# A row of edge scores made by VectorE transposes and broadcast transfers, and a first pair of plain products, in a two-layer graph attention kernel on Trainium2

## Chip, cores and metric

One core of one Trainium2 chip runs the whole kernel. Its engines work side by side, each through its own instructions in order: TensorE (PE, with its weight loads PEld), VectorE (DVE), ScalarE (ACT), GpSimd (POOL) and SyncE (SP), which issues nearly all transfers. The metric is the device time of one launch in microseconds (us); less is better.

## What is computed

x has 128 graphs of 128 nodes with 512 features; adj holds, for each graph, a 128x128 matrix of zeros and ones. Layer 0 is masked attention with eight heads of 64, layer 1 a graph attention with one head. Each layer adds its input and normalizes each node's features.

```python
# layer 0
q, k, v = x @ Wq + bq, x @ Wk + bk, x @ Wv + bv            # 8 heads of 64
attn = softmax(where(adj > 0, q @ k.T / 8, -1e9))          # per graph and head
x = layernorm(x + relu((attn @ v) @ Wo + bo))
# layer 1
Wh = x @ W
e = leaky_relu((Wh @ a1)[:, :, None] + (Wh @ a2)[:, None, :], 0.2)   # e_i + e_j
attention = softmax(where(adj == 0, -1e9, e))              # per graph
x = layernorm(x + elu(attention @ Wh))
```

All of it is float32.

## The kernel before

**Pairs.** Two graphs make a pair; there are 64 pairs, numbered p. The two graphs of a pair are the two row halves of one 256x512 matrix, and each of the products by Wq and Wk (`qk0` to `qk6`), Wv (`v0` to `v6`), Wo (`o0` to `o6`) and W (`w0` to `w6`) is a 2x2 block product with seven block products instead of eight. For that the blocks of the left side are added up by GpSimd (`x_sums`, `o_sums`, `z_sums`: four additions each, in `left_sums`), and the blocks of the weights once at the start (`sums_qk`, `sums_v`, `sums_o`, `sums_w`). The seven products share three PSUM banks, A, B and C: `PRODUCTS` lists for each the bank, the left block and the weight block. A product that adds to a bank has to wait until the partial sum in it has been read. The reads are called by the tag and the part: `qk_p1` and `qk_p1q` (ScalarE) read bank A after product 0, `qk_p6` and `qk_p7` (VectorE) read B after products 1 and 3, and `c11`, `c22`, `c21`, `c12` write the four blocks of the result. The same names with `v_`, `o_` and `w_` stand for the other three weights. For qk the 128x512 output takes eight 128x128 matmuls a product (each shows as two records); for v, o and w a product is two 128x256 matmuls.

**Steps of a pair.** `load_blocks` loads x in blocks (`xb`) and `x_transpose0/1` transposes it on VectorE into `xT`. After `qk` and `v` come `logits` (TensorE), `mask_logits0/1` and `max_logits0/1` (VectorE), `exp_logits`, `norm_logits` (ScalarE), and the transpose of the attention weights: `weights_t` (VectorE, 32x32 blocks, tile `prb`), `weights_out` (to HBM, `prd`) and `weights_in` (back as `prT`). `mix_values` (TensorE, tile `po`) and `mix_values_out` (ScalarE) lead to `o`, then `residual0`, `stats0`, `mean0`, `rstd0`, `shift0`, `norm0`. Layer 1 uses (attention @ x) @ W. W @ a1 and W @ a2 are folded at the start: `fold_a` (keys `sums_fold0/1`, 8 products on VectorE after a load of one half of `a` issued by GpSimd), `fold_t` (TensorE, `pwa`), `fold_out` (ScalarE, `wa_bc`). `edge_term0i` and `edge_term1i` (VectorE, L506) give the node columns e_i and e_j, `edge_row` makes a row of the column e_j, and then come `edge_sums` (ScalarE, L525), `edge_leaky`, `edge_mask`, `edge_max` (VectorE), `edge_exp`, the transpose `edges_t`, `edges_t_out`, `edges_t_in` (tiles `atb`, `atd`, `attT`), `mix_nodes` (TensorE, `pz`), `mix_nodes_out`, the products of `w`, the elu (`elu_exp`, `elu_low` on GpSimd, `elu_max`), `residual1`, the second normalization and `store`. The last pair transposes with TensorE instead of through HBM (`ppT`, `pat`).

**The row before.** The column is broadcast to 128 columns and transposed by TensorE into PSUM:

```python
for i in range(2):
    nc.tensor.transpose(ST["j", p][:, i, :], ej[:, i:i + 1].to_broadcast([P, P]), ident)
```

**The order.** It is written out by hand. `PLAN` gives each step a time, `PERIOD` the distance of two pairs, and all steps of all pairs are sorted by p * PERIOD + PLAN[key]; the numbers set only the order, in which every engine then gets its own instructions. In the steady state TensorE works on the products of several pairs in turn: `qk` and `v` of pair p+1 stand near `o` of pair p-1 and `w` of pair p-3. `BUFS` gives the number of buffers of each tile. One PSUM bank (tag `ps`, one buffer) is shared by `po`, `pj`, `pz` and `pwa`. The steps `sums_...` run once.

Of the kernel before, what the change touches and what calls it, by code (L numbers as in the profile page):

```python
# [14 lines left out]
N_BATCH = 128  # L15


PERIOD = 75.72
PLAN = dict(
    load_blocks=-145.14, x_transpose1=-53.4, x_transpose0=-35.51, sums_qk=-33.34, sums_fold1=-29.39, qk0=-27.1,  # L20
    x_sums=-23.88, qk_p1=-23.14, qk1=-22.39, fill_logits0=-21.87, qk_p1q=-21.45, qk2=-21.2, qk_c11=-20.29,
    qk_p6=-19.48, sums_v=-18.68, qk3=-17.99, load_adj=-17.97, mask=-17.48, qk_p7=-16.28, qk4=-15.67, qk5=-15.2,
    qk_c22=-12.6, qk6=-10.28, v0=-9.3, qk_c21=-4.36, qk_c12=-1.71, v_p1=-1.71, logits=0.0, fill_logits1=0.47,
    mask_logits0=2.51, max_logits0=3.23, v1=3.74, v2=5.42, v_p6=9.86, v3=10.28, mask_logits1=11.03, v_c11=11.14,
    v4=11.19, v_p7=11.39, v5=11.72, max_logits1=11.91, v_c22=12.76, exp_logits0=13.09, v6=13.11, v_c21=17.62,
    v_c12=24.79, sum_logits0=38.24, exp_logits1=39.15, sums_fold0=44.28, sum_logits1=44.73, norm_logits0=46.84,
    sums_fold_t1=51.88, sums_fold_out1=51.93, weights_t0=52.11, sums_fold_t0=54.57, norm_logits1=54.59,
    weights_t1=56.92, weights_out0=69.01, sums_fold_out0=71.24, weights_out1=72.35, weights_in0=73.55,
    mix_values0=75.07, mix_values_out0=75.62, weights_in1=76.59, mix_values1=77.67, sums_w=80.78,
    mix_values_out1=82.2, sums_o=82.43, o_sums=83.08, load_x1=83.6, fill_edges=94.56, o0=106.33, o_p1=107.8,  # L30
    o1=110.7, o_p6=113.29, o4=114.99, o3=115.54, o_p1l=115.68, o_p7=116.85, o2=117.07, o5=117.95, load_x0=119.48,
    o_c11=123.99, o_c22=124.53, o6=125.56, o_c21=125.62, residual01=129.31, o_c12=132.6, stats01=134.5,
    mean01=136.37, rstd01=136.65, shift01=136.91, residual00=138.02, stats00=142.08, mean00=142.88, norm01=143.34,
    rstd00=143.95, shift00=146.71, edge_term01=147.04, edge_term11=147.54, norm00=147.98, edge_term10=152.41,
    edge_term00=152.98, edge_row=160.06, edge_sums=163.14, edge_leaky=163.47, edge_mask=167.08, edge_max=171.62,
    edge_exp=173.19, edges_t=179.68, edges_t_out=188.05, edges_t_in=199.52, mix_nodes1=209.13,
    mix_nodes_out1=213.74, mix_nodes0=214.15, mix_nodes_out0=221.07, z_sums=225.48, w0=238.82, w_p1=240.45,
    w1=248.86, w2=249.67, w_p6=251.97, w3=255.0, w_c11=255.99, w_p7=256.03, w4=256.11, w_c22=259.18, w5=259.7,
    w6=259.92, edge_norm=261.55, w_c21=261.61, w_c12=264.14, elu_exp1=276.85, elu_low1=281.16, elu_exp0=304.17,
    elu_low0=304.34, elu_max0=329.44, elu_max1=330.72, residual10=333.57, stats10=338.98, mean10=339.98,  # L40
    residual11=340.94, rstd10=361.09, shift10=363.8, stats11=376.92, mean11=380.35, rstd11=388.98, shift11=391.45,
    finish0=399.29, store0=407.37, finish1=407.57, store1=460.65)

ENDS = {}

BUFS = dict(
    xb=2, adj=4, xT=2, sx=1, e1a512=1, e1b512=1, u2512=1, pr=2, mask=1, u3512=1, qT=2, kT=2, e1a256=2, t=2, scr=1,
    cw=6, u2256=1, u3256=2, cv=2, prb=2, x=2, prT=2, oT=2, so=1, e1b256=1, co=6, at=2, e=1, atb=1, attT=1, zT=2,
    sz=1)


@with_exitstack
def tile_two_graph_layers(ctx: ExitStack, tc: tile.TileContext, x, adj, wq, bq, wk, bk, wv, bv, wo, bo, w, a, out,
# [8 lines left out]
    nc = tc.nc  # L62
    P = 128
# [43 lines left out]
    make_identity(nc, ident)  # L107
    half = const.tile([P, 1], F32, tag="half", name="half")
    nc.gpsimd.memset(half, -0.5)

# [179 lines left out]
        left_sums("x", p, XT)  # L290

    def qk_product(p, j):
        if j == 0:
            BL["qk", p] = Blocks("qk", p, D)
        columns_product(BL["qk", p], wqk, "x", j)

    def with_bias(dst, src, bias):
        for f in range(NC):
            nc.scalar.activation(dst[:, f * P:(f + 1) * P], src[:, f * P:(f + 1) * P], AF.Identity,
                                 bias=bias[:, f:f + 1], scale=1.0)  # L300

    def qk_p1(p):
        b = BL["qk", p]
        b.e1k, b.e1q = b.tile("e1a"), b.tile("e1b")
        with_bias(b.e1k, b.bank["A"], bk_sb)

    def qk_p1q(p):
        b = BL["qk", p]
        with_bias(b.e1q, b.bank["A"], bqs)

    def qk_p6(p):
        b = BL["qk", p]
        b.u2 = b.tile("u2")
        nc.vector.tensor_add(b.u2, b.bank["B"], b.e1k)  # L314

# [183 lines left out]
    def edge_term(b, s):  # L499

        p, i = b // 2, b % 2
        store = (EI, EJ)[s]
        if p not in store:
            store[p] = small.tile([P, 2], F32, tag=f"e{s}", name=f"e{s}_{p}")
        scr = buf([P, D], F32, "scr", f"scr{s}_{b}")
        nc.vector.scalar_tensor_tensor(scr, X1[b], 1.0, wa_bc[s], op0=ALU.mult, op1=ALU.mult,  # L506
                                       accum_out=store[p][:, i:i + 1])


    def edge_row(p):  # L510

        ej = EJ.pop(p)
        ST["j", p] = ps.tile([P, 2, P], F32, tag="ps", name=f"pj_{p}")
        for i in range(2):
            nc.tensor.transpose(ST["j", p][:, i, :], ej[:, i:i + 1].to_broadcast([P, P]), ident)
# [5 lines left out]
    def edge_sums(p):  # L521
        e = ST["e", p] = buf([P, 2, P], F32, "e", f"e_{p}")
        j, ei = ST.pop(("j", p)), EI.pop(p)
        for i in range(2):
            nc.scalar.activation(e[:, i, :], j[:, i, :], AF.Identity, bias=ei[:, i:i + 1], scale=1.0)  # L525
# [168 lines left out]
```

## Time and profile before

| what | value |
|---|---|
| median of 3 runs | 2439.42 us (2438.52 to 2440.8) |
| the profiled execution | 2441.85 us, span 2440.1 us |
| mean granted TensorE clock | 0.990 |
| VectorE busy | 1881.5 us (77%) |
| ScalarE busy | 1570.9 us (64%) |
| GpSimd busy | 1497.0 us (61%) |
| TensorE busy in the first 40 us | 10.95 us |
| TensorE busy from 200 to 600 us | 400.00 us |
| TensorE busy in the last 60 us | 37.63 us |
| `pj` (L515) | 128 matmuls, 25.1 us busy, mean 278 ns |
| L506 (`edge_term`) | 128x512, 256 times, median 692 ns, at most 1253 ns |

A line of a timeline reads: start, us from first start to last end, engine, line of the kernel, operation, output <- inputs, shapes, count, and in brackets the idle time before it with what ended it. TensorE's instructions overlap: the time that one takes from the next is the distance of two starts. A line of waits reads: engine, tile and line that waited, what it waited for, total, times, longest. A line of transfer issues ends with the size of one and the median time from issue to landing.

### The profile page before, as it was taken

How to read it: one execution, taken by the hardware profiler on the slowest of the kernel's cores; microseconds unless marked ns; L12 is line 12 of the kernel's file. 1: busy time of each engine (PE TensorE's matmuls, PEld its weight loads, DVE VectorE, ACT ScalarE, POOL GpSimd, SP SyncE). 2: the span in 40 equal slices, each digit the busy share in tenths (PEclk: the TensorE clock that was granted, in tenths of full speed). 3: DMA queues.
4: the chain of work that ended last, by engine and by line, in shares of the span. 5: the costliest groups of instructions: out<-in, count | busy, mean ns of one | idle time of the engine just before them, and what ended most of it. 6: DMA issues, size and time to landing. Idle time of an engine off the chain costs nothing. (4 is left out here: it accounts for less than half of the span.)

```text
span 2440.1 us, 51873 instructions
## 1 busy us (share of the span) xinstructions
PE 2383.7 (98%) x17818; PEld 2156.8 (88%) x17818; DVE 1881.5 (77%) x3838; ACT 1570.9 (64%) x5510; POOL 1497.0 (61%) x1989
## 2 busy tenths in 40 slices
PE   4999999999999999999999999999999999999996
PEld 4899899899899998998998998998998989989985
DVE  4777877877877877877778778778778778778786
ACT  2666666667667666666666666666666676676674
POOL 1445665666666666666666656656656666666657
PEclk8999999999999999999999999999999999999998
DMA  5443443443443443443443444434434434434421
GB/s 130 113 107 101 108 120 104 114 120 97 118 123 92 118 126 93 115 121 101 112 118 99 120 113 104 120 108 110 120 100 115 122 92 119 127 92 116 121 82 53
DMA packets 305766, 267.14 MB, mean 109 GB/s; under 512 B 89760, under 2 KB 255392, under 8 KB 305504
## 3 DMA queue, kind: packets, MB, share of 16 engines
q1 hardware_dynamic: 304528, 261.98, 40.4%
q8 instruction: 143, 2.34, 0.4%
q10 hardware_dynamic: 640, 1.05, 0.2%
q14 instruction: 119, 0.97, 0.1%
q0 software_dynamic: 336, 0.79, 0.1%
HBM read 155.85 MB, written 107.87 MB: 108 GB/s over the span
## 5 line engine op out<-in xcount | busy, mean ns | idle before, releaser
L425 ACT ACTIVATE pr<-pr,nmax 128x128 f32<-128x128 f32 x1024 | 394.9, 393 | 0.0
L434 ACT ACTIVATE pr<-pr,tot 128x128 f32<-128x128 f32 x1024 | 314.6, 412 | 106.6 <-DVE tot L429 106.6
L271 POOL TENSOR_SCALAR rstd<-mv 128x1 f32<-128x1 f32 x256 | 112.0, 437 | 319.7 <-DVE mv L268 310.2
L604 POOL TENSOR_TENSOR cw<-cw,co 128x512 f32<-128x512 f32 x126 | 184.3, 1482 | 163.2 <-DVE cw L601 163.2
L255 PE MATMUL pBqk<-sx,wqk 128*128 128x128 f32 x2048 | 253.1, 277 | 18.6 <-issue 13.7
L255 PEld LDWEIGHTS pBqk<-sx,wqk 128*128 128x128 f32 x2048 | 247.0, 194 | 22.1 <-issue 18.9
L255 PE MATMUL pAqk<-xT,wqk 128*128 128x128 f32 x2048 | 251.9, 277 | 13.2 <-DVE xT L286 10.5
L598 POOL TENSOR_SCALAR t<-t 128x512 f32<-128x512 f32 x126 | 245.4, 1948 | 31.5 <-ACT t L594 31.5
L279 ACT ACTIVATE co<-co,nmean,rstd 128x512 f32<-128x512 f32 x128 | 104.2, 814 | 246.8 <-DVE kT L330 216.8
L255 PEld LDWEIGHTS pAqk<-xT,wqk 128*128 128x128 f32 x2048 | 245.8, 193 | 17.2 <-DVE xT L286 10.5
L255 PE MATMUL pCqk<-sx,wqk 128*128 128x128 f32 x2048 | 250.6, 276 | 0.0
L255 PEld LDWEIGHTS pCqk<-sx,wqk 128*128 128x128 f32 x2048 | 240.0, 193 | 0.0
L484 ACT ACTIVATE oT<-po,bv 128x128 f32<-128x128 f32 x512 | 146.3, 368 | 123.2 <-PE po L475 123.2
L506 DVE SCALAR_TENSOR_TENSOR scr<-co,wa_bc 128x512 f32<-128x512 f32 x256 | 201.8, 788 | 8.4 <-ACT co L279 3.2
L425 ACT ACTIVATION_READ_ACCUMULATOR pr<-pr,nmax 128x1 f32 x1024 | 198.1, 193 | 0.0
L444 DVE STREAM_TRANSPOSE prb<-pr 128x1024 f32<-128x1024 f32 x126 | 156.2, 1239 | 49.4 <-ACT pr L434 49.4
L410 POOL MEMSET pr<- 128x1024 f32 x128 | 121.6, 951 | 99.8 <-DVE prb L444 99.8
L414 DVE COPY_PREDICATED pr<-mask,s 128x1024 f32<-128x1024 int32 x128 | 173.1, 1352 | 4.3 <-PE s L402 4.2
L272 POOL TENSOR_TENSOR rstd<-rstd,half 128x1 f32<-128x1 f32 x256 | 159.5, 623 | 21.3
L419 DVE TENSOR_REDUCE nmax<-pr 128x8 f32<-128x1024 f32 x128 | 155.4, 1214 | 2.2
L314 DVE TENSOR_TENSOR u2qk<-pBqk,e1aqk 128x512 f32<-128x512 f32 x64 | 44.2, 690 | 144.3 <-PE pBqk L255 141.6
L150 POOL TENSOR_TENSOR sx<-sx,xT 128x256 f32<-128x256 f32 x63 | 46.1, 732 | 175.6 <-DVE xT L286 175.5
(155 smaller groups left out, 6144.1 us busy)
## 6 DMA issues: line engine op xcount, KB each, us to landing
prd<-prb SPq DMA_DIRECT2D x126, 512.0 KB, 2.9
prT<-prd SPq DMA_DIRECT2D x504, 128.0 KB, 3.6
xb<-in_x_dram SPq DMA_DIRECT2D x256, 128.0 KB, 4.3
x<-in_x_dram SPq DMA_DIRECT2D x128, 256.0 KB, 3.7
out_dram<-cw SPq DMA_DIRECT2D x128, 256.0 KB, 2.0
adj<-in_adj_dram SPq DMA_DIRECT2D x64, 128.0 KB, 2.3
atd<-atb SPq DMA_DIRECT2D x63, 128.0 KB, 1.8
attT<-atd SPq DMA_DIRECT2D x252, 32.0 KB, 1.9
```

The lines of the kernel that those rows point to most:

```text
L255: nc.tensor.matmul(out[:, f * P:(f + 1) * P], weight[:, b_i, c, f * P:(f + 1) * P], left_block(left, blk.pair, a_i, c), start=first and f ...
L272: nc.gpsimd.tensor_tensor(RSTD[key], RSTD[key], half, op=ALU.pow)
L410: nc.gpsimd.memset(PR[b], NEG)
L414: nc.vector.copy_predicated(PR[b], MASK[p][:, i, :].unsqueeze(1).to_broadcast([P, H, P]), ST.pop(("s", b)).rearrange("p j h k -> p (j h) k"))
L419: nc.vector.tensor_reduce(NMAX[b], PR[b], AX.X, ALU.max, negate=True)
L425: nc.scalar.activation(PR[b][:, h, :], PR[b][:, h, :], AF.Exp, bias=nmax[:, h:h + 1], scale=1.0, accum_out=TOT[b][:, h:h + 1])
L434: nc.scalar.activation(PR[b][:, h, :], PR[b][:, h, :], AF.Copy, scale=tot[:, h:h + 1])
L444: nc.vector.transpose(PRB[b].rearrange("p k h s -> p h k s"), PR.pop(b).rearrange("p h (k r) -> p h k r", r=32))
L484: nc.scalar.activation(OT[b][:, f, :], po[:, f, :], AF.Identity, bias=bv_sb[:, f:f + 1], scale=1.0)
L506: nc.vector.scalar_tensor_tensor(scr, X1[b], 1.0, wa_bc[s], op0=ALU.mult, op1=ALU.mult, accum_out=store[p][:, i:i + 1])
L598: side_engine(b // 2).tensor_scalar(t, t, 1.0, -1.0, op0=ALU.min, op1=ALU.add)
L604: side_engine(b // 2).tensor_tensor(Y[b], Y[b], X1.pop(b), op=ALU.add)
```

## The change

The two transposes of `edge_row` on TensorE go. The columns e_j are now accumulated into columns 0 and 32 of one of three 128x64 tiles that were filled with zeros once (`ej_blocks`); `edge_blocks` transposes such a tile in 32x32 blocks on VectorE, so that four partitions (0, 32, 64, 96) hold the row in pieces of 32 for both graphs; `edge_row` then issues four transfers on SP, each of which copies 64 numbers of one partition to all 128 partitions, 256 bytes each. `edge_sums` reads the row from SBUF instead of PSUM. For pair 0, Q and K come from eight plain products in four steps (`qk0` to `qk3`) in banks A, B, C and a fourth bank D, with the bias added by ScalarE when a product is read; `sums_qk` and `x_sums` are not needed for them. `PLAN`, `PERIOD` and `BUFS` are new, and with them the order of all steps: among others `sums_qk` and `sums_fold0` come later, `qk4` before `qk2`, `v1` before `mix_values0`, `v3` before `v2`, `edge_term00` between `mask_logits0` and `max_logits0`, and `weights_t1` after `qk1`.

```diff
@@ -15,38 +15,38 @@
 N_BATCH = 128
 
 
-PERIOD = 75.72
+PERIOD = 78.77
 PLAN = dict(
...
-    finish0=399.29, store0=407.37, finish1=407.57, store1=460.65)
+    load_adj=-214.28, load_blocks=-156.46, x_transpose0=-118.96, x_transpose1=-64.06, qk0=-36.02, x_sums=-35.84,
+    qk1=-32.98, qk_p1=-31.71, fill_logits0=-31.52, sums_v=-30.63, qk4=-28.65, qk_p6=-28.53, qk_p1q=-27.7,
+    qk2=-26.32, qk_c11=-24.89, qk3=-22.63, v0=-21.4, qk_p7=-19.94, qk_c22=-19.93, qk5=-14.75, qk6=-13.44,
+    qk_c21=-7.89, qk_c12=-7.85, sums_fold1=-6.69, v_p1=-4.73, v1=-4.54, fill_logits1=-1.85, mask=-1.24, v_p6=-0.29,
+    logits=0.0, mask_logits0=2.0, max_logits0=3.74, sums_fold_t1=4.13, v3=4.41, v_p7=4.43, v2=7.45, v4=9.21,
+    v_c11=9.21, mask_logits1=10.04, load_x1=10.32, v5=13.29, v_c22=14.67, exp_logits0=14.75, v_c21=15.09, v6=17.23,
+    v_c12=17.58, max_logits1=22.12, sum_logits0=24.06, norm_logits0=27.41, exp_logits1=33.3, sums_qk=38.84,
+    weights_t0=43.7, sum_logits1=43.78, sums_fold_out1=45.25, sums_fold0=46.53, norm_logits1=52.01,
+    weights_out0=53.62, weights_t1=55.61, sums_fold_t0=63.24, weights_out1=68.01, weights_in0=70.44,
+    sums_fold_out0=71.92, weights_in1=74.3, mix_values0=75.85, sums_w=78.52, mix_values_out0=80.72,
+    mix_values1=81.43, mix_values_out1=85.44, load_x0=87.17, sums_o=94.72, o_sums=101.64, o0=106.22, o_p1=113.64,
+    o1=113.67, o4=115.87, o_p6=116.22, o_p1l=117.15, o3=117.16, o_p7=117.32, o2=117.77, o_c11=118.24, o_c22=118.29,
+    o5=120.85, o6=121.7, o_c21=121.88, o_c12=122.76, residual01=122.76, stats01=122.82, mean01=123.85,
+    residual00=127.73, rstd01=128.28, shift01=128.77, stats00=130.31, norm01=131.24, mean00=131.45, rstd00=133.98,
+    edge_term01=134.39, shift00=135.59, edge_term11=137.39, norm00=140.45, edge_term10=144.28, edge_blocks=146.15,
+    fill_edges=152.96, edge_row=155.48, edge_term00=159.96, edge_sums=163.39, edge_leaky=169.07, edge_mask=175.0,
+    edge_max=179.3, edge_exp=184.85, edges_t=185.93, edges_t_out=188.28, edges_t_in=189.77, mix_nodes1=211.95,
+    mix_nodes_out1=218.25, mix_nodes0=220.51, mix_nodes_out0=222.79, z_sums=231.06, w0=248.23, edge_norm=250.39,
+    w_p1=253.84, w1=254.02, w2=254.75, w_p6=256.75, w3=258.71, w_c11=259.13, w4=262.95, w_p7=264.55, w5=268.2,
+    w_c22=268.29, w6=268.5, w_c21=269.01, w_c12=270.9, elu_exp1=288.36, elu_exp0=298.97, elu_low1=307.12,
+    elu_max1=314.12, elu_low0=326.19, elu_max0=338.66, residual10=340.21, stats10=349.64, mean10=349.96,
+    residual11=350.83, rstd10=358.93, stats11=386.25, mean11=395.88, shift10=413.33, rstd11=414.6, shift11=416.7,
+    finish0=436.56, finish1=440.87, store0=451.59, store1=492.12)
 
 ENDS = {}
 
 BUFS = dict(
-    xb=2, adj=4, xT=2, sx=1, e1a512=1, e1b512=1, u2512=1, pr=2, mask=1, u3512=1, qT=2, kT=2, e1a256=2, t=2, scr=1,
...
-    sz=1)
+    xb=2, adj=5, xT=3, t=2, scr=1, cw=6, sx=1, pr=2, qT=2, kT=2, mask=2, e1a256=1, u2256=1, cv=2, u3256=1, prb=1,
+    e1a512=1, e1b512=1, u2512=1, u3512=1, prT=2, oT=2, so=1, x=3, at=1, e1b256=1, co=6, ejr=1, e=1, atb=1, attT=1,
+    zT=2, sz=1)
 
 
 @with_exitstack
@@ -107,6 +107,10 @@
     make_identity(nc, ident)
     half = const.tile([P, 1], F32, tag="half", name="half")
     nc.gpsimd.memset(half, -0.5)
+
+    ej_blocks = [const.tile([P, 64], F32, tag=f"ej{k}", name=f"ejb_{k}") for k in range(3)]
+    for t in ej_blocks:
+        nc.gpsimd.memset(t, 0.0)
 
 
 
@@ -290,9 +294,29 @@
         left_sums("x", p, XT)
 
     def qk_product(p, j):
-        if j == 0:
+        if p == 0:
+            if j < 4:
+                qk_plain(j)
+            return
+        if ("qk", p) not in BL:
             BL["qk", p] = Blocks("qk", p, D)
         columns_product(BL["qk", p], wqk, "x", j)
+
+    def qk_plain(j):
+
+        if j == 0:
+            b = BL["qk", 0] = Blocks("qk", 0, D)
+            for bank in "ABC":
+                b.psum(bank)
+            b.bank["D"] = ps.tile([P, D], F32, tag="ps", name="pDqk_0")
+        banks, half, b_i = (("AB", 0, 0), ("AB", 1, 1), ("CD", 0, 5), ("CD", 1, 2))[j]
+        for i, bank in enumerate(banks):
+            out = BL["qk", 0].bank[bank]
+            for f in range(NC):
+                for c in range(2):
+                    nc.tensor.matmul(out[:, f * P:(f + 1) * P], wqk[:, b_i, c, f * P:(f + 1) * P],
+                                     left_block("x", 0, 2 * i + half, c), start=half == 0 and f == 0 and c == 0,
+                                     stop=half == 1 and f == NC - 1 and c == 1, skip_group_check=True)
 
     def with_bias(dst, src, bias):
         for f in range(NC):
@@ -301,15 +325,20 @@
 
     def qk_p1(p):
         b = BL["qk", p]
+        if p == 0:
+            return
         b.e1k, b.e1q = b.tile("e1a"), b.tile("e1b")
         with_bias(b.e1k, b.bank["A"], bk_sb)
 
     def qk_p1q(p):
         b = BL["qk", p]
-        with_bias(b.e1q, b.bank["A"], bqs)
+        if p:
+            with_bias(b.e1q, b.bank["A"], bqs)
 
     def qk_p6(p):
         b = BL["qk", p]
+        if p == 0:
+            return
         b.u2 = b.tile("u2")
         nc.vector.tensor_add(b.u2, b.bank["B"], b.e1k)
 
@@ -322,24 +351,35 @@
 
     def qk_p7(p):
         b = BL["qk", p]
+        if p == 0:
+            return
         b.u3 = b.tile("u3")
         nc.vector.tensor_add(b.u3, b.bank["B"], b.e1k)
 
     def qk_c22(p):
         b = BL["qk", p]
-        nc.vector.tensor_add(QK["k", 2 * p + 1], b.bank["C"], b.u3)
+        if p == 0:
+            with_bias(QK["k", 1], b.bank["D"], bk_sb)
+        else:
+            nc.vector.tensor_add(QK["k", 2 * p + 1], b.bank["C"], b.u3)
 
     def qk_c21(p):
         b = BL["qk", p]
-        nc.vector.tensor_add(QK["q", 2 * p + 1], b.bank["B"], b.e1q)
+        if p == 0:
+            with_bias(QK["q", 1], b.bank["B"], bqs)
+        else:
+            nc.vector.tensor_add(QK["q", 2 * p + 1], b.bank["B"], b.e1q)
 
     def qk_c12(p):
         b = BL["qk", p]
-        nc.vector.tensor_add(QK["k", 2 * p], b.bank["C"], b.u2)
+        if p == 0:
+            with_bias(QK["k", 0], b.bank["C"], bk_sb)
+        else:
+            nc.vector.tensor_add(QK["k", 2 * p], b.bank["C"], b.u2)
 
     def half_product(tag, p, j):
 
-        if j == 0:
+        if (tag, p) not in BL:
             BL[tag, p] = Blocks(tag, p, HALF)
         weight, left = dict(v=(wv_b, "x"), o=(wo_b, "o"), w=(w_b, "z"))[tag]
         rows_product(BL[tag, p], weight, left, j)
@@ -499,20 +539,24 @@
     def edge_term(b, s):
 
         p, i = b // 2, b % 2
-        store = (EI, EJ)[s]
-        if p not in store:
-            store[p] = small.tile([P, 2], F32, tag=f"e{s}", name=f"e{s}_{p}")
+        if s == 0 and p not in EI:
+            EI[p] = small.tile([P, 2], F32, tag="ei", name=f"ei_{p}")
+        acc = ej_blocks[p % 3][:, 32 * i:32 * i + 1] if s else EI[p][:, i:i + 1]
         scr = buf([P, D], F32, "scr", f"scr{s}_{b}")
-        nc.vector.scalar_tensor_tensor(scr, X1[b], 1.0, wa_bc[s], op0=ALU.mult, op1=ALU.mult,
-                                       accum_out=store[p][:, i:i + 1])
-
+        nc.vector.scalar_tensor_tensor(scr, X1[b], 1.0, wa_bc[s], op0=ALU.mult, op1=ALU.mult, accum_out=acc)
+
+
+    def edge_blocks(p):
+
+        EJ[p] = small.tile([P, 64], F32, tag="ej", name=f"ej_{p}")
+        nc.vector.transpose(EJ[p], ej_blocks[p % 3])
 
     def edge_row(p):
 
+        ST["j", p] = buf([P, 4, 64], F32, "ejr", f"ejr_{p}")
         ej = EJ.pop(p)
-        ST["j", p] = ps.tile([P, 2, P], F32, tag="ps", name=f"pj_{p}")
-        for i in range(2):
-            nc.tensor.transpose(ST["j", p][:, i, :], ej[:, i:i + 1].to_broadcast([P, P]), ident)
+        for v in range(4):
+            nc.sync.dma_start(ST["j", p][:, v, :], ej[32 * v:32 * v + 1, :].unsqueeze(1).to_broadcast([1, P, 64]))
 
     def fill_edges(p):
         AT[p] = buf([P, 2, P], F32, "at", f"at_{p}")
@@ -522,7 +566,8 @@
         e = ST["e", p] = buf([P, 2, P], F32, "e", f"e_{p}")
         j, ei = ST.pop(("j", p)), EI.pop(p)
         for i in range(2):
-            nc.scalar.activation(e[:, i, :], j[:, i, :], AF.Identity, bias=ei[:, i:i + 1], scale=1.0)
+            nc.scalar.activation(e[:, i, :].rearrange("p (v s) -> p v s", s=32), j[:, :, 32 * i:32 * i + 32],
+                                 AF.Identity, bias=ei[:, i:i + 1], scale=1.0)
 
     def edge_leaky(p):
         e = ST["e", p]
@@ -624,7 +669,7 @@
         if p > 1:
             at("load_adj", p, load_adj, p)
             at("load_blocks", p, load_blocks, p)
-        for fn in (edge_row, fill_edges, edge_sums, edge_leaky, edge_mask, edge_max, edge_exp,
+        for fn in (edge_blocks, edge_row, fill_edges, edge_sums, edge_leaky, edge_mask, edge_max, edge_exp,
                    edge_norm, edges_t, edges_t_out, edges_t_in):
             at(fn.__name__, p, fn, p)
         at("x_sums", p, x_sums, p)
```

More of the change, by code (lines that the diff above doesn't have):

```diff
@@ L15 @@
 N_BATCH = 128
-PERIOD = 75.72
+PERIOD = 78.77
 PLAN = dict(
[L20 to L41, printed above, removed]
-    finish0=399.29, store0=407.37, finish1=407.57, store1=460.65)
@@ L44 @@
+    elu_max1=314.12, elu_low0=326.19, elu_max0=338.66, residual10=340.21, stats10=349.64, mean10=349.96,
+    residual11=350.83, rstd10=358.93, stats11=386.25, mean11=395.88, shift10=413.33, rstd11=414.6, shift11=416.7,
+    finish0=436.56, finish1=440.87, store0=451.59, store1=492.12)
 ENDS = {}
 BUFS = dict(
-    xb=2, adj=4, xT=2, sx=1, e1a512=1, e1b512=1, u2512=1, pr=2, mask=1, u3512=1, qT=2, kT=2, e1a256=2, t=2, scr=1,
-    cw=6, u2256=1, u3256=2, cv=2, prb=2, x=2, prT=2, oT=2, so=1, e1b256=1, co=6, at=2, e=1, atb=1, attT=1, zT=2,
```

## The prediction

> **What bounds the kernel now.** I read the page's busy shares first, then its slices, TensorE's waits, and timelines of the start, of one pair in the middle and of the end.
>
> ```profile
> PE 2383.7 (98%) x17818; PEld 2156.8 (88%) x17818; DVE 1881.5 (77%) x3838; ACT 1570.9 (64%) x5510; POOL 1497.0 (61%) x1989
> PE   4999999999999999999999999999999999999996
> ```
>
> TensorE is the bound: every slice but the first and the last is full. Three things can matter: fewer TensorE instructions in the middle, a shorter start or end, new holes in the middle. Its waits (engine, line, releaser: total, times, longest):
>
> ```profile
> PE pBqk L255 <- issue: 13.7, 1, 13.7
> PE pAqk L255 <- DVE xT L286: 10.5, 1, 10.5
> PE pBqk L255 <- DVE wqk L130: 4.8, 1, 4.8
> ```
>
> Three waits at the start hold 29.0 us. The rest of the list is some 15 us, nearly all in the first 115 us and the last 65. The middle, on TensorE's timeline:
>
> ```profile
> 1028.21 1.03 PE L244 MATMUL pAv<-wv,xT 128*128 128x256 f32 x4
> 1029.08 0.38 PE L515 MATMUL pj<-ident,e 128*128 128x128 f32 x2
> 1029.30 1.03 PE L244 MATMUL pBv<-wv,sx 128*128 128x256 f32 x4
> ```
>
> Starts count here, since ends overlap. The two transposes of `edge_row` take 1029.30 - 1029.08 = 0.22 us of a pair's 36.94 (`e1bo` of `o_p1` starts at 1001.26 and again at 1038.20).
>
> **Part 1: the row leaves TensorE.** 62 of the 64 `pj` lie in the full stretch: 62 x 0.22 = 13.6 us less; the other two belong to the tail (part 3). What replaces them:
> - VectorE: one 128x64 stream transpose. The nearest row is the 128x256 one, 0.44; by width 0.15. VectorE is 77% busy and waits for TensorE just behind it (`qk_c21`), so it costs nothing; uncovered, at most 62 x 0.44 = 27.
> - SP: four issues at 0.45 (`attT`'s four take 1.80) of 32 KB each. The nearest landing has the same size in pieces of 128 B (last number: us to landing):
>
> ```profile
> attT<-atd SPq DMA_DIRECT2D x252, 32.0 KB, 1.9
> ```
>
> The Trainium skill, "DMA: Bandwidth & Descriptors", Specifications, speaks against the transfers: pieces under 512 B are read, modified and written instead of moved at line rate, and these have 256 B. The `attT` row, with smaller pieces, shows no such delay; were each landing doubled by it, 3.8, the wait below would still be hidden.
>
> Is the row in time? I laid the changed order along TensorE's start-to-start times of this trace (0.86 a 128x256 product, 1.79 an eight-matmul 128x128 one, 0.89 `pz`, 1.03 `po`, 1.99 `logits`). From a pair's `logits` at 0: `po` 2.0, `v3` 3.0, `v2`, `v4`, `w0` 5.7, `v5` 6.6, `v6` 7.4, six of w and `o0`, `o1` 14.3, `o5` 17.8, `qk0` 18.6, `o6`, `qk1` 21.3, `qk4`, `qk2` 24.8, `pz`, `qk3`, `v0` 29.3, `pz`, `qk5`, `qk6`, `v1` 34.6, `po` 35.5, end 36.7. ScalarE: `qk_p1` and `qk_p1q` to 22.6, `norm_logits1` (2.4) to 25.0; `weights_t1` to 26.4; its write takes 2.9, so `weights_in1` is issued to 31.5. `edge_blocks` ends at 31.6. The broadcasts are issued 31.6 to 33.4 and land near 35. ScalarE's `edge_sums` stands at 1.2 of the next period (37.9), behind `mix_values_out0`. Behind it wait `mix_values_out1`, `v_c11`, and through that `w0` at 5.7: a broadcast may take 7 us to land before `w0` is late. The slowest `xb` load took 6.5. What SP issues behind it (`load_blocks`, two `load_x`) moves by 1.8 and is needed 15 later.
>
> **Part 2: the first pair.** Before, VectorE's queue decided: `sums_fold1` waited for W in front of `qk_p6`, so product 4 of 7 started at 38.82, at half pace.
>
> ```profile
> 22.41 2.66 PE L255 MATMUL pAqk<-xT,wqk 128*128 128x128 f32 x16
> 38.82 3.75 PE L255 MATMUL pBqk<-sx,wqk 128*128 128x128 f32 x16 [13.75 <-issue]
> 75.52 1.09 PE L475 MATMUL po<-prT,cv 128*64 128x128 f32 x16
> ```
>
> ```profile
> 36.09 0.43 DVE L207 SCALAR_TENSOR_TENSOR wa_scr<-w,a_bc 128x256 f32<-128x256 f32 x1 [1.36 <-DMA w<-in_L_gnn_W_dram]
> 38.03 0.68 DVE L314 TENSOR_TENSOR u2qk<-pBqk,e1aqk 128x512 f32<-128x512 f32 x1
> ```
>
> After, the plain products need only both `xT` and Wq, Wk (the last Wk was there at 17.49): start 9.9, about 23 records at 0.22 and 105 at 0.11, end 27. The extra product (1.79) falls into time that was idle. But `sums_fold1` still stands on VectorE ahead of `mask`, `v_p6` and `mask_logits0`, and W comes when it came: TensorE does `v0`, `v1`, `logits` to about 33, and the rest starts at 38.0. Each step by its row:
> - VectorE: mask 0.2, `v_p6` 0.4, `mask_logits0` 1.4, max 1.1, `v_p7` 0.3, `mask_logits1` 1.3, `v_c22` 0.4. TensorE, cold: `pwa`, `v3` to `v6`, end 45.2.
> - VectorE's max to 46.9; ScalarE normalizes (2.4) to 49.5, second exp (3.1) to 52.6. GpSimd: `x_sums` of pair 1 to 48.2, and only then the load of the second row of `a`, which took 5.8 to land: 54.0. `sums_fold0` 4.2, `qk_p6` 0.6: 58.8.
> - `qk3` of pair 1 at 58.9, `v0`, `pwa`, `qk5`, `qk6`, `v1` (1.79 + 0.86 + 0.44 + 1.79 + 1.79 + 0.86 = 7.5): `po` of pair 0 at 66.5.
>
> Before, `po` stood at 75.52 with `v1` still to come. Gain 75.52 + 0.86 - 66.5 = 9.9. If the row of `a` lands earlier, the exponentials (52.8) decide: +1.2; if half pace hits `qk1` to `qk3` and `prT` (3.6 to land) holds `po`: -3. So 7 to 11.
>
> **Part 3: the tail.** Before, TensorE stood for `po` (1.38), `po` (1.68), `pj` (1.24) and later 3.76 at the last `pj`, ahead of `w0`. After, the last `ppT` and `pz` alternate and nothing stands ahead of `w0`: pair 61's w may start up to 3.6 earlier. But the last pair's row needs four issues and a landing (3.7) where `pj` took 0.5; part of that is covered by w, so 0.8 to 2.5 later. Gain -2 to 3.5; taken 1.5.
>
> **Part 4: the new order in the middle.** Where VectorE gates TensorE, a margin of 0.17 between its end and the product's start was free (`v_c22` 1032.58, `v6` 1032.75), 0.16 cost 0.07 (`w_p6` 1035.18, `w3` 1035.34). After, by the same sums, most margins are 0.18 to 0.26 and `qk0`'s is 0.14: about as before. But one step meets GpSimd. VectorE from `mask_logits0` (1.27 after `logits`, as at 49.64 and 50.91): 1.33, 0.10, `edge_term00` 0.73, max 1.13, `v_p7` 0.34, `mask_logits1` 1.33, so `edge_leaky` at 6.24. GpSimd's four `o_sums` start 2.37 after the second `po` (1026.22, 1028.59), at 4.4, 5.2, 5.9 and 6.6. A two-input VectorE operation that meets such a sum is held until it ends; the normal `edge_leaky` took 0.42, the last one
>
> ```profile
> 2410.91 0.79 DVE L529 SCALAR_TENSOR_TENSOR e<-e 128x256 f32<-128x256 f32 x1 [0.66 <-ACT e L525]
> 2410.70 0.72 POOL L152 TENSOR_TENSOR sz<-zT,sz 128x256 f32<-128x256 f32 x1
> ```
>
> So `edge_leaky` is held by the third sum: worth 6.5; `edge_norm` and `v_c22` follow, to 7.38; `v6` at 7.42 needs 0.16: 0.12 lost a pair, x 62 = 7.4 us. Ends: 0 (it comes before 5.9) and the first rival.
> `edge_term01` and `11` meet `elu_low1`: the one like case (L491 beside L598) took 1.02 instead of 0.66. 0.7 for both, hidden by the wait for `qk3`. The Trainium skill, "SBUF — State Buffer", has the loser of the shared port wait for the whole other instruction, which would be 1.7 and almost all of that cover; the row did not.
>
> **Sum.** 13.6 + 9.9 + 1.5 - 7.4 = 17.6. The profiled execution was 2441.85 (span 2440.1), 2.4 above the median 2439.42: 2424.2 for it, 2421.8 for the median.
>
> **Rivals.**
> - Slower: `edge_leaky` comes after 6.6 and is held by the fourth sum to 7.2. Then `v_c22` ends at 8.07 and `v6` loses 0.81 a pair, x 62 = 50: 2439 - 25 + 50 = 2464. It decides from 0.36 us of lateness in VectorE. For: `edge_term00` took 1.09, not 0.69, beside GpSimd's sums before. Against: here only 128x1 operations run beside it. 0.15.
> - Only part 1 counts, since W and the row of `a` set the start: 13.6 + 1.5 - 7.4 = 7.7, 2432. For: 38.03 stays. Against: what follows it is shorter. 0.12.
> - The broadcast lands after 7 us: each us more costs 62; at 8 it is 2484. Against: 1.9. 0.03.
> - My forecast, own range 2409 to 2430: 0.70.
>
> **Numbers.** Median 2421.8. Low end: start 11, no held `edge_leaky`, tail 3.5: 2411, and 3 for what I overlooked: 2408. High end: past 2432, to 2440, until two in ten are out. The runs lie within 2.3 us, so 0.2% (4.9) can be told from no change. Faster, from the forecast and half of the second rival: 0.76; within 0.2%: 0.06; slower: 0.18.
>
> **What would show it.** No `pj`; 36.7 to 36.9 between two `logits`; `edge_sums` without a wait for a DMA; `po` of pair 0 near 66.5; `edge_leaky` longer than 0.42 in every pair. I am wrong if TensorE's waits list `w0`, `v6` or `qk0` some sixty times beyond 0.2, or if the second row of `a` does not gate `sums_fold0`.

## The result, and the profile after

The changed kernel takes 2425.58 us (median of 4 runs, 2423.96 to 2427.27), the kernel before on the same chip 2440.11 (4 runs): 0.9941 times as long, 95% interval 0.9924 to 0.9958, 14.5 us less. The forecast was 2421.8 in 2408 to 2440. The profiled execution took 2427.27 with a span of 2425.5; before, 2441.85 and 2440.1. Both profiles lie 1.7 us above their medians, so their difference, 14.6, is close to that of the medians.

The page's busy shares and TensorE's slices:

```profile
PE 2375.7 (98%) x17706; PEld 2149.5 (89%) x17706; DVE 1846.5 (76%) x3897; ACT 1558.2 (64%) x5514; POOL 1473.9 (61%) x1992
PE   6999999999999999999999999999999999999996
```

TensorE is still the bound, and only the two end slices are not full. So the span can be cut at the starts of `logits`, one per pair: the stretch to the fourth, the sixty periods from there to the last, and the end. The forecast's terms are put on the same cuts (`v1` of the next pair now stands ahead of `logits`, so its 0.86 us counts less for the start and more for the end; the two pairs outside the sixty make up the end's last 0.2).

| stretch | before | after | change | forecast |
|---|---|---|---|---|
| start to the fourth `logits` | 137.56 | 129.72 | -7.8 | -9.0 |
| 60 periods | 2217.08 | 2204.12 | -13.0 | -6.0 |
| last `logits` to the end | 85.46 | 91.66 | **+6.2** | -2.6 |
| span | 2440.1 | 2425.5 | -14.6 | -17.6 |

That the sum came out near the forecast is luck: two wrong terms had opposite signs. The middle gained 7 us more, the end was 8.8 us worse.

TensorE's waits (engine, tile, line, releaser: total, times, longest), the five largest:

```profile
PE pAqk L317 <- DVE xT L290: 10.0, 1, 10.0
PE pz L625 <- ACT zT L630: 7.8, 3, 4.1
PE pwa L221 <- DVE wa_rep L215: 5.8, 1, 5.8
PE pAw L248 <- ACT e1aw L395: 4.1, 2, 3.0
PE pBqk L259 <- DVE wqk L134: 3.5, 1, 3.5
```

None comes sixty times: the middle has no hole. `pAqk`, `pwa` and `pBqk` belong to the start, `pz` (its 4.1 and 2.9) and `pAw` to the end. The first two pairs on TensorE's timeline:

```profile
31.23 2.06 PE L442 MATMUL s<-kT,qT 64*128 64x128 f32 x32
39.06 1.11 PE L221 MATMUL pwa<-ident,wa_rep 128*128 128x128 f32 x4 [5.78 <-DVE wa_rep L215]
...
51.25 3.75 PE L259 MATMUL pBqk<-sx,wqk 128*128 128x128 f32 x16 [3.47 <-DVE wqk L134]
...
67.27 1.09 PE L515 MATMUL po<-prT,cv 128*64 128x128 f32 x16
```

`po` of pair 0 stands at 67.27 (forecast 66.5, before 75.52). In the middle, four lines of ScalarE, VectorE and GpSimd (one fence each), where the forecast had put a collision; `logits` of this pair started at 1011.34:

```profile
1014.58 0.69 ACT L569 ACTIVATE e<-ejr,ei 128x128 f32<-128x128 f32 x2 [1.98 <-DVE scr L546]
```

```profile
1017.16 0.41 DVE L574 SCALAR_TENSOR_TENSOR e<-e 128x256 f32<-128x256 f32 x1
```

```profile
1016.38 0.73 POOL L153 TENSOR_TENSOR so<-oT 128x256 f32<-128x256 f32 x1 [0.73 <-ACT oT L524]
1017.19 0.97 POOL L154 TENSOR_TENSOR so<-so,oT 128x256 f32<-128x256 f32 x1
```

`edge_sums` waits for e_i (`scr` of `edge_term00`), not for the row. `edge_leaky` is not held: it starts first, and the GpSimd sum that starts 0.03 later takes 0.97 instead of 0.73.

The broadcast in the page's issues (last number: median from issue to landing), and the end on ScalarE's timeline:

```profile
ejr<-ej SPq DMA_DIRECT2D x256, 32.0 KB, 3.9
```

```profile
2385.35 0.56 ACT L630 COPY zT<-pz 128x512 f32<-128x512 f32 x1
...
2394.61 0.69 ACT L569 ACTIVATE e<-ejr,ei 128x128 f32<-128x128 f32 x2 [5.96 <-DMA ejr<-ej]
2395.21 0.35 ACT L395 COPY e1aw<-pAw 128x256 f32<-128x256 f32 x1
```

VectorE had the row's blocks at 2388.20. SP issued the four transfers from 2388.23 to 2390.64, and the last landed at 2394.5: 6.4 us from block to read. ScalarE stood for 5.96 of them, and behind `edge_sums` on it `e1aw`, which TensorE's third w product needs. TensorE through that stretch (length, busy and records, granted clock, share of the transfers, GB/s):

```profile
2385.00:2390.00 5.00, 3.36 (x11) 0.50 0.06 3
2390.00:2395.00 5.00, 2.66 (x6) 0.50 0.54 75
2395.00:2400.00 5.00, 4.38 (x10) 0.50 0.01 2
```

It is not only waiting, it also works at half clock, from 2384.6 to 2401.7 by the profile's clock records.

### The profile page after: what moved, and what is told of

It is laid out like the page before. It is cut to its first block, busy times and chain, and to the rows that moved or that the text cites. A ratio compares the mean times of both kernels' runs of the same rounds, so it can differ in the third digit from the quotient of the medians.

```text
span 2425.5 us, 51781 instructions
## 1 busy us (share of the span) xinstructions
PE 2375.7 (98%) x17706; PEld 2149.5 (89%) x17706; DVE 1846.5 (76%) x3897; ACT 1558.2 (64%) x5514; POOL 1473.9 (61%) x1992
## 3 DMA queue, kind: packets, MB, share of 16 engines
q10 hardware_dynamic: 640, 1.05, 0.2%
## 5 line engine op out<-in xcount | busy, mean ns | idle before, releaser
L649 POOL TENSOR_TENSOR cw<-cw,co 128x512 f32<-128x512 f32 x126 | 157.6, 1272 | 235.9 <-DVE cw L646 235.9
L275 POOL TENSOR_SCALAR rstd<-mv 128x1 f32<-128x1 f32 x256 | 101.4, 396 | 294.1 <-DVE mv L272 288.7
L643 POOL TENSOR_SCALAR t<-t 128x512 f32<-128x512 f32 x126 | 276.1, 2192 | 0.1
L259 PE MATMUL pAqk<-xT,wqk 128*128 128x128 f32 x2016 | 245.5, 275 | 0.0
L259 PEld LDWEIGHTS pAqk<-xT,wqk 128*128 128x128 f32 x2016 | 235.9, 192 | 7.4
L546 DVE SCALAR_TENSOR_TENSOR scr<-co,wa_bc 128x512 f32<-128x512 f32 x256 | 173.4, 677 | 4.1 <-ACT co L283 1.9
L276 POOL TENSOR_TENSOR rstd<-rstd,half 128x1 f32<-128x1 f32 x256 | 144.8, 566 | 21.3
L625 PE MATMUL pz<-attT,co 128*128 128x128 f32 x1024 | 136.3, 276 | 7.8 <-ACT zT L630 7.8
L515 PE MATMUL po<-prT,cv 128*64 128x128 f32 x2048 | 141.8, 281 | 1.9 <-ACT oT L524 1.2
L248 PE MATMUL pBv<-wv,sx 128*128 128x256 f32 x512 | 139.1, 394 | 2.0 <-DVE wv L134 2.0
```

The lines of the kernel that those rows point to most:

```text
L259: nc.tensor.matmul(out[:, f * P:(f + 1) * P], weight[:, b_i, c, f * P:(f + 1) * P], left_block(left, blk.pair, a_i, c), start=first and f ...
L276: nc.gpsimd.tensor_tensor(RSTD[key], RSTD[key], half, op=ALU.pow)
L515: nc.tensor.matmul(ST["o", b][j * DH:(j + 1) * DH, hp, :], v[:, h * DH:(h + 1) * DH], prT[:, :, j * (H // 2) + hp, :], start=True, stop=True)
L643: side_engine(b // 2).tensor_scalar(t, t, 1.0, -1.0, op0=ALU.min, op1=ALU.add)
L649: side_engine(b // 2).tensor_tensor(Y[b], Y[b], X1.pop(b), op=ALU.add)
```

## The experiments

All are edits of the changed kernel, and their times are compared with its 2425.58; the kernel before, timed again beside them, had medians of 2439.9 to 2440.5. Where a stretch is named, it is one of the table's, from each kernel's profile.

**1. The last row by the product** (`row_last_pe`)

```diff
     def edge_row(p):
+        if p == n_pair - 1:
+            ST["j", p] = ps.tile([P, 2, P], F32, tag="ps", name=f"pj_{p}")
+            for i in range(2):
+                col = ej_blocks[p % 3][:, 32 * i:32 * i + 1]
+                nc.tensor.transpose(ST["j", p][:, i, :], col.to_broadcast([P, P]), ident)
+            return
```

> Only the last pair's row goes back to two TensorE transposes; the other 63 pairs keep the broadcast. Theory (the end is longer because, with no work beside it, the broadcast's own time counts: the transposed column was ready at 2388.20 and `edge_sums` read the row at 2394.61, 6.4 us, where the product needed 1.2): now `edge_sums` of the last pair waits only for `edge_term00`, which ends at 2391.1, so it starts 3.4 us earlier and the median falls by 3 to 4.5 us, to about 2421.5; the second-to-last pair's part stays. Rival (the end is longer because `zT` is copied behind `norm01` on ScalarE and TensorE runs at half clock): 0 to -1 us.

Measured: 2420.62 (2420.37 to 2421.3), 5.0 less, a little more than the theory's 3 to 4.5; the end 86.01 instead of 91.66. ScalarE's timeline of this kernel:

```profile
2385.13 0.56 ACT L642 COPY zT<-pz 128x512 f32<-128x512 f32 x1
...
2390.97 0.63 ACT L578 ACTIVATE e<-pj,ei 128x128 f32<-128x128 f32 x2 [2.52 <-PE pAw L248]
```

`edge_sums` is 3.4 us earlier against the copy of `zT` (5.84 after it instead of 9.26), and TensorE is back at full clock earlier: 0.80 on average from 2390 to 2395, 1.00 after. The line names `pAw`, which `edge_sums` does not read; it needs e_i, and `edge_term00` on VectorE, behind an `elu_max`, ended at 2390.88. The broadcast in the last pair costs 5.0 us by the medians. By these two profiles it is 5.65 of the end's 6.2, but single profiles scatter: in the nine that keep the broadcast, experiment 2 among them, the end takes 89.8 to 92.5, with 10.2 to 17.1 us of half clock at that place, and in the three with the product of experiments 1 and 9 85.7 to 86.3, with 6.8 to 10.2.

**2. The copies of `zT` first** (`zt_first`)

```diff
-ENDS = {}
+ENDS = {-2: dict(mix_nodes1=-5.0, mix_nodes_out1=-9.0)}
```

> The changed kernel, but in the second-to-last pair `mix_nodes_out1` (the copy of `zT`) stands ahead of `norm01` of the last pair on ScalarE. Theory (the broadcast's time is the cost): the second `pz` starts near 2382.6 instead of 2385.96 and `w0` near 2385.4 instead of 2388.7, but `e1aw` is still copied behind `edge_sums`, which waits for the row: 0 to -1.5 us. Rival (the order on ScalarE and the half clock after the 4.1 us wait are the cost): -4 to -6 us, to about 2420.5.

Measured: 2425.95, the end 91.57. The wait of `pz` for `zT` fell from 4.14 to 0.73, and the time came back one product later:

```profile
2382.18 1.16 PE L625 MATMUL pz<-attT,co 128*128 128x128 f32 x8 [0.73 <-ACT zT L630]
2387.91 2.08 PE L248 MATMUL pAw<-w,zT 128*128 128x256 f32 x4 [4.57 <-ACT zT L630]
```

So the 4.1 us in the second wait of the list cost nothing by themselves: the other copy of `zT` still stands behind `norm00` of the last pair on ScalarE, the row comes when it came, and TensorE only waits in another place. The rival is out; experiments 1 and 2 tell the broadcast and this order on ScalarE apart.

**3. Two idle transposes more in every pair** (`two_more`)

```diff
         ST["o", b] = ps.tile([P, H // 2, P], F32, tag="ps", name=f"po_{b}")
+        if b % 2 == 0 and b // 2 < n_pair - 2:
+            for i in range(2):
+                nc.tensor.transpose(ST["o", b][:, i, :], ident, ident)
```

> The changed kernel with two 128x128 transposes of the identity more on TensorE in each of the first 62 pairs (into the region that `mix_values` overwrites), read by nobody; the result is the reference's. Theory (TensorE sets the pace and the gain in the middle is the 0.22 us of `pj`): the period goes from 36.735 to 36.95, 62 x 0.22 = +13.6 us, a median near 2439. Rival (the gain came from the new order of the work): less than +4 us.

Measured: 2438.55 (11 runs), 13.0 more. The sixty periods take 2217.06 instead of 2204.12, and before the change 2217.08: 36.951 each again. 59 of them hold the two transposes, so these are 0.219 us, ahead of `mix_values` as at the old place of `pj`, and all of it shows. The gain of the middle is `pj`, not the plan.

**4. Seven products for the first pair** (`seven_first`, then `seven_early`)

```diff
     def qk_product(p, j):
-        if p == 0:
-            if j < 4:
-                qk_plain(j)
-            return
...
-    sums_qk=38.84
+    sums_qk=-37.0
```

> Only the eight plain products are undone: the first pair's Q and K by seven products again, with `sums_qk` ahead of them on VectorE; the new order (with `sums_fold1` behind the reads of Q and K) stays. Theory (the start gained by the order, since TensorE waited for W and for VectorE's queue from 33 to 39 and from 48 to 51 anyway): first `logits` near 40 instead of 31.2, but `po` of pair 0 near 67 to 70 instead of 67.3, so 0 to +3 us. Rival (the plain products themselves gave the start's 9 us): `po` near 76, +9 us.

Measured: 2437.09, 11.5 more, `po` of pair 0 at 77.49. This would speak for the rival, but the edit had a flaw of its own: at -37 `sums_qk` stood behind the second pair's `x_transpose0` on VectorE, which waits for a load, and TensorE waited 17.7 us for the sums:

```profile
28.09 0.71 DVE L290 STREAM_TRANSPOSE xT<-xb 128x512 f32<-128x512 f32 x1 [13.29 <-DMA xb<-in_x_dram]
28.73 1.18 DVE L133 TENSOR_TENSOR wqk<-wqk 128x1024 f32<-128x1024 f32 x1
```

With `sums_qk=-45.0`, ahead of that transpose:

> As seven_first, but `sums_qk` stands ahead of the second pair's first `x_transpose` on VectorE too, which waits for a load until 28.1 and held the sums until 28.7 in seven_first. The sums now run from about 17.5 to 22.7, and `qk1` starts near 19 instead of 31.3. `u2` of the first pair still stands behind that transpose (28.8), so the first `logits` come near 38.5 and `wa_rep` near 42. Theory A (seven products cost only what VectorE's sums delay; with the sums early the start is as good as with plain products, since `sums_qk` is then out of VectorE's way at 48 to 53): `po` of pair 0 at 66 to 70, a median of 2424 to 2429. Theory B (the plain products themselves carry the start's gain, whatever stands where): `po` near 76, a median of 2434 or more.

Measured: 2432.30 (2431.44 to 2433.61), `po` at 71.81. Neither theory holds alone. Of the 8.25 us by which `po` came earlier than before, 3.7 come with the new order and seven products (75.52 to 71.81), 4.5 with the plain products (71.81 to 67.27). That holds for this place of `sums_qk`; whether seven products do better with another was not tried.

**5. The folds of `a` out of the start** (`folds_late`, then `start_parts`)

```diff
-sums_qk=38.84, sums_fold1=-6.69, sums_fold_t1=4.13, sums_fold0=46.53, sums_fold_t0=63.24
+sums_qk=18.0, sums_fold1=90.0, sums_fold_t1=100.0, sums_fold0=103.0, sums_fold_t0=112.0
```

> The changed kernel with both folds of `a` (`sums_fold*`) moved behind `mix_values` of pair 0, where VectorE and TensorE's `ps` bank are free, and `sums_qk` up to the end of the first pair's v reads. Theory (the rest of the start is VectorE's queue: TensorE waited 5.8 us for `wa_rep` and 3.5 for `wqk`, and ran at half clock after): both waits go or fall under 1.5, `qk1` of pair 1 starts near 42.5 instead of 51.3, `po` of pair 0 near 59 to 61 instead of 67.3: -6 to -9 us, a median of 2417 to 2420. Rival (the softmax chain of pair 0 or the transfers of its weights set `po`): 0 to -3 us.

Here the folds read a block of W that `sums_w` has already overwritten, so `wa_bc` and all that follows from it have other values; the instructions are the same. Measured: 2438.19, 12.6 more. The two waits shrank or moved (3.5 became 2.0, not under 1.5; `pwa` left the start, but its second one waits 4.3 at 85.47) and `qk1` stood at 41.95 instead of 51.25. And TensorE's waits have two new lines:

```profile
PE pAqk L259 <- ACT e1bqk L323: 8.2, 1, 8.2
...
PE pCv L248 <- DVE cv L424: 4.6, 1, 4.6
```

`e1b` of pair 1 stands behind two softmax steps of pair 0 on ScalarE, which had waited for VectorE's sums: `po` at 64.94, only 2.3 earlier. And the fold at its new place took 5 us of VectorE just ahead of `v_c22` of pair 1, where TensorE is full. For `start_parts` each fold was cut into five pieces, placed where VectorE was seen idle and ahead of `sums_w`, and `sums_qk` put behind `sum_logits0`:

> The changed kernel with the order of the start changed alone: each fold of `a` cut into five pieces that stand where VectorE was idle in folds_late, all of them ahead of `sums_w` (moved behind `shift00`), so nothing is left out; `sums_qk` right behind `max_logits1` and `sum_logits0` of pair 0, so that ScalarE's second softmax isn't held by it. Theory (the start's remaining cost is the order of VectorE's queue, and through it ScalarE's): the v products follow `logits` at once, `qk1` of pair 1 starts near 43 instead of 51.3, `e1bqk` is there by 48, `po` of pair 0 near 60 instead of 67.3, -5 to -8 us, a median of 2418 to 2420. Rival (another piece of the start gates, the transfers of the weights or ScalarE): -1 to -3 us.

Measured: 2423.68 (2421.75 to 2423.96), 1.9 less, short of the 5 to 8. In its profile `po` is at 60.59, as expected, and 5.0 us are left of that at the fourth `logits`. That profile is the fastest of its five runs, and the changed kernel's the slowest of its four, so 5 is the upper end. With the same first instructions, `po` of pair 0 lay between 65.7 and 67.3 from kernel to kernel; how much of the gap is that scatter is open.

**6. e_i earlier** (`term_early`)

```diff
-edge_term00=159.96
+edge_term00=157.4
```

> The changed kernel with `edge_term00` moved ahead of `mask_logits0` in every pair, so that `edge_sums` no longer waits 1.98 us on ScalarE for e_i; the second `oT` and with it the four GpSimd sums of `o_sums` begin 0.7 us earlier after `logits` (4.3 instead of 5.04), which is where the prediction had them. Theory (the prediction missed that wait, and its collision of `edge_leaky` with a GpSimd sum is real): `edge_leaky` meets a sum and takes 0.6 to 0.9 instead of 0.41, and the period grows by up to 0.12 us, 0 to +7 us. Rival (no such collision costs TensorE anything): a period of 36.70 to 36.75, within 2 us of the changed kernel.

Measured: 2424.05, the period 36.733. With `logits` at 1010.04, GpSimd's sums begin 4.35 behind it, `edge_leaky` 5.75 behind it:

```profile
1015.79 0.42 DVE L574 SCALAR_TENSOR_TENSOR e<-e 128x256 f32<-128x256 f32 x1
```

```profile
1015.20 0.73 POOL L154 TENSOR_TENSOR so<-so,oT 128x256 f32<-128x256 f32 x1
1015.89 0.90 POOL L155 TENSOR_TENSOR so<-oT,oT 128x256 f32<-128x256 f32 x1
```

It meets the last 0.14 us of a sum and is not held; the next sum is. That is so in most pairs. In eight pairs of the middle the sums begin 0.10 to 0.34 us later, and there `edge_leaky` is held for 0.51 to 0.76, as in this one (`logits` at 1450.84):

```profile
1456.59 0.76 DVE L574 SCALAR_TENSOR_TENSOR e<-e 128x256 f32<-128x256 f32 x1
```

```profile
1456.34 0.73 POOL L154 TENSOR_TENSOR so<-so,oT 128x256 f32<-128x256 f32 x1
```

The next `logits` follow at 1487.58, a period of 36.73 as in the pairs without it; `v_c22` is done at 6.9 after `logits`, and `v6` needs it at 7.4. So the theory's collision is real, and the rival is right about its price: none. `edge_sums` now waited 0.27 us for the row, which was there 1.5 us after `logits`.

**7. An order made for the end** (`tail_order`), on top of experiment 1

```diff
-ENDS = {}
+ENDS = {-2: dict(mix_nodes1=-8.0, mix_nodes_out1=-13.0, mix_nodes0=-15.0, mix_nodes_out0=-16.0, w0=-16.0),
+        -1: dict(edge_term00=-15.0, edge_leaky=-5.07, edge_mask=-10.0, edge_max=-13.3, edge_exp=-14.85, edges_t=-10.2,
+                 edges_t_in=-13.3, mix_nodes1=-26.0, mix_nodes_out1=-28.25, mix_nodes0=-30.3, mix_nodes_out0=-32.2,
+                 z_sums=-40.0)}
```

> As row_last_pe (the last pair's row by two TensorE transposes), and in the last two pairs the order is made for the end: both copies of `zT` of pair 62 ahead of `norm01` and `norm00` of pair 63 on ScalarE, `w0` ahead of the row, `edge_term00` ahead of `elu_max`, the edge softmax and `pat` of pair 63 ahead of `w2` of pair 62, `pz` among the last w products. Theory (after row_last_pe what is left of the end is TensorE's holes while the layer norm runs, and about 2 us of half clock behind them): the waits of `pz` for `zT` fall from 4.1 and 2.9 to 0.7, `edge_sums` starts 2.3 us earlier, TensorE ends 2 to 4 us earlier than in row_last_pe, a median near 2417.5. Rival (the layer norm of the last pair and the w products behind it set the end whatever the order): within 1 us of row_last_pe's 2420.6.

Measured: 2428.34, 7.7 more than experiment 1. With `pat` ahead of `w2`, TensorE waited for the softmax instead of working (1.91). Two normalizations and two elu steps now stood ahead of the last `e1aw` on ScalarE (1.14), and on VectorE an `elu_max` that waited for GpSimd stood ahead of the last `u2w` (2.45), after which three w products ran at half clock. The last pair shows the collision at its longest here: `edge_leaky` starts with 0.57 us of a GpSimd sum to go and takes twice as long.

```profile
2390.29 0.85 DVE L590 SCALAR_TENSOR_TENSOR e<-e 128x256 f32<-128x256 f32 x1
```

```profile
2389.69 1.17 POOL L160 TENSOR_TENSOR sz<-zT,sz 128x256 f32<-128x256 f32 x1
```

**8. The broadcast twice** (`row_twice`)

```diff
+        dsts = [ST["j", p]]
+        if p < n_pair - 2:
+            dsts.insert(0, buf([P, 4, 64], F32, "ejr2", f"ejr2_{p}"))
+        for dst in dsts:
             for v in range(4):
```

> The changed kernel with the four broadcasts of the row issued twice in each of the first 62 pairs, first into a tile that nobody reads, then into `ejr`; the last two pairs keep one. The row that is read lands some 2.4 us later (four issues at 0.60), and SP's queue holds `xb` and `x` back by as much. In term_early `edge_sums` could read the row 1.5 us after `logits`, in the changed kernel it starts at 3.24 anyway, behind e_i. Theory (in the middle the broadcast is hidden, only where the work runs out does its time count): `edge_sums` starts at 3.2 to 4.2 us after `logits`, waits for the row 0 to 1 us, the period stays at 36.73 to 36.75, a median within 2 us of 2425.6. Rival (the row's transfers or SP's queue gate TensorE when they come later): a period of 36.8 or more, +4 us and up.

Measured: 2517.07 (2513.09 to 2517.89), 91 more; the period 38.20 instead of 36.735. The theory's number is refuted, and the rival is right about the row's transfers. A pair of this kernel (`logits` at 1048.77), on SP, ScalarE and TensorE:

```profile
1043.99 6.83 SPq L563 DMA_DIRECT2D ejr<-ej  x8
```

```profile
1054.12 0.69 ACT L573 ACTIVATE e<-ejr,ei 128x128 f32<-128x128 f32 x2 [4.09 <-DMA ejr<-ej]
1054.72 1.11 ACT L524 ACTIVATE oT<-po,bv 128x128 f32<-128x128 f32 x4
1055.72 0.38 ACT L415 COPY cv<-pAv 128x256 f32<-128x256 f32 x1
```

```profile
1056.15 1.13 PE L248 MATMUL pAw<-w,zT 128*128 128x256 f32 x4 [1.51 <-ACT cv L415]
```

Eight issues took 6.83 us where four took 2.41, so the last issue ended 4.4 later, not 2.4. `edge_sums` read it 5.35 us after `logits` instead of 3.24, `mix_values_out1` and `v_c11` stand behind it on ScalarE, and `w0` behind `v_c11`: the very queue that the forecast named. In the list of TensorE's waits this one comes 61 times, 67.8 us in all. In this pair 2.1 us of lateness at `edge_sums` cost TensorE 1.5, so the middle hides the broadcast with a reserve of about 0.6 us there and 1.7 more in the wait for e_i.

**9. What pays, together** (`row_term`, `best`): experiment 1 with the `edge_term00` of experiment 6, and both with `start_parts`.

> row_last_pe (the last pair's row by two TensorE transposes) with `edge_term00` ahead of `mask_logits0` in every pair, as in term_early. In row_last_pe the last `edge_sums` waited for `edge_term00`, behind an `elu_max` on VectorE, until 2390.97, with the row there at 2389.2. Expected: the row read 1.5 to 2.3 us earlier, the stretch from the last `logits` to the end 84 to 85 instead of 86.0, the period unchanged at 36.73, a median of 2418 to 2419.5. Rival (the w products behind the row set the end): 2420 to 2421.

> start_parts and row_term together: the two ends do not touch each other, so their gains add: 2425.6 - (5 to 8) - (6 to 7.5), a median of 2410 to 2414.5, against 2440 before the change.

Measured: `row_term` 2420.19, within 0.5 of experiment 1, as its rival had it. Its `edge_term00` still stands behind the same `elu_max1` of pair 61 on VectorE (plan time 156.6 against 157.4), so the row is read at the same 2.47 us after `pj`; the end is 85.68. `best` 2419.16 (2417.77 to 2420.2), 0.9913 of the kernel before (0.9899 to 0.9926), 6.4 less than the changed kernel. Nearly all of it is experiment 1; the start's 1.0 beside `row_term` can't be told from scatter.

## Why the prediction was right or wrong

**Part 1, right.** 0.22 us a pair: measured 36.951 - 36.735 = 0.216, and put back by experiment 3. The transpose on VectorE (0.25) cost nothing, as forecast. SP's four issues cost nothing either, but with far less room than thought.

**The row's price, wrong.** The row `attT` (32 KB each, 1.9 us to land, 0.45 an issue) was taken as the neighbour; measured are 3.9 (3.1 to 5.5) and 0.60. The Trainium skill, "DMA: Bandwidth & Descriptors", Specifications, had spoken for slower transfers below 512 B. Doubling the neighbour gave 3.8, and that number came, but no run shows that the size of the pieces is the reason: `attT` has still smaller ones and landed in 1.8. The same page, Why small descriptors are slow (HBM only), exempts transfers from SBUF to SBUF, which `ejr` is. Another difference is that each `ejr` transfer reads one partition 128 times. In the middle the wrong price did no harm; at 7 us to land the forecast saw `w0` late, and experiment 8 shows that rival's mechanism at work, with the row some 4 us later.

**Part 3, wrong: the term that was mis-sized.** The end was to be 1.5 us shorter and is some 7 longer (6.2, and 0.86 for `v1`). The forecast had 0.8 to 2.5 for the row, because 3.7 less 0.5 would partly be covered by w. Measured are 6.4 from block to read (1.8 to the start of the last issue, 4.5 from there to its landing), and little covers it: `w0` and `w1` run, then `w2` needs `e1aw`, which stands behind `edge_sums` on ScalarE, and TensorE stands for 2.96. The forecast had named exactly that queue for the middle (`v_c11`, `w0`) and not asked for it at the end. Experiment 1 puts 5.0 of it on the broadcast by the medians, 5.65 by the profiles. The hoped-for gain ahead of `w0` did not come: the waits moved to `pz`, and experiment 2 shows that the longest of them does not set the end. What is left without the broadcast, 1.4 (86.01 against 85.46 less the 0.86 of `v1`), was not traced further.

**Part 4, wrong.** No 0.12 us a pair is lost. Two steps failed. `edge_sums` needs e_i as well as the row, and `edge_term00` now comes behind `mask_logits0`; the wait of 1.98 on ScalarE moves the second `oT`, and `o_sums` begin 5.04 after `logits` and not 4.4. And VectorE was 0.4 faster along its steps: `edge_leaky` at 5.82, not 6.24. So it met the start of the second sum instead of the middle of the third. With the wait gone (experiment 6) it met the last 0.14 of a sum in most pairs, and nothing was lost. The premise that a sum holds it is right: experiments 6 and 7 show it. The price is not: in the eight held pairs of experiment 6 `v_c22` ended at least 0.5 us before `v6` needed it, where the forecast had 0.04, and the period stayed at 36.73.

**Part 2, right in size, not in the gate.** Forecast 9.9 at `po`, measured 75.52 + 0.86 - 67.27 = 9.1, of which 0.4 was lost again before the fourth `logits`. `u2qk` of pair 1 ended at 59.4, forecast 58.8. But the second row of `a` was issued at 49.97 and landed 3.66 later, at 53.62, and VectorE came to `sums_fold0` only at 54.53: its own queue, with `sums_qk` from 48.19 to 53.3 in it, was the gate and not the load, a sign of being wrong that the forecast had named itself. The forecast's 54.0 for the landing came near because a late issue (48.2 expected) and a fast load (5.8 expected) cancel. The 3.47 of `qk1` for these sums was not in the forecast. The rival that only part 1 counts is out.

## What to carry to other kernels

Price a moved step at each place where it runs: the same broadcast was free in sixty pairs, cost about 5 us once in the last pair, where little covered it, and 1.5 us a pair as soon as the reserve of some 2 us in the middle was used up. For each instruction that now waits, list all its operands and what is queued behind it on its engine, at the end of the kernel as well as in the middle. A forecast near the result is no proof of its terms: compare stretch by stretch before believing any of them.

## What the hardware showed beside this

- Four of these broadcasts took 0.60 us of SP each. Eight in a row held it for 6.26 (median of 62 pairs, 6.83 in the one shown): in the median the first four take 0.48 to 0.60, the fifth and sixth 0.97 and 1.02. It need not be the broadcast itself: in the changed kernel the `xb` loads right behind the four broadcasts take as long (0.95 and 1.05 at 1009.0 and 1010.0).
- TensorE stayed at half clock from 2384.6 to 2401.7 although it worked 10.4 of the 15 us from 2385 to 2400. The Trainium skill, "TensorE: Matmul & The Clock Gate", Part 1, gives about 3.4 us of sustained work until full rate. In this profile full clock came 6.1 us after the last wait (2395.61 to 2401.7); at the same place it came after 2.8 to 3.4 in `two_more`, `term_early` and `folds_late`.
- Of a VectorE operation with two SBUF inputs and a GpSimd sum that meet, the later one is held. In all 24 cases of the fourteen profiles in which `edge_leaky` (0.42 alone) was held for more than 0.5, it ended 0.28 us after the end of the sum; so it loses nothing when less than 0.14 of the sum is left. The other way round, L154 took 0.24 more and L155 0.17 more when they started 0.03 and 0.10 after `edge_leaky`.
